# Ranks of equal keys counted at the end of diffusion step 1, and step 2 begun with its logits

## The chip, the core and the metric

The kernel runs on one core of one Trainium2 chip. The metric is the device time of one execution in microseconds (us); shown times are medians over several executions. The engines are named as in the profile: PE is TensorE's matmul, PEld its weight load, DVE is VectorE, ACT is ScalarE, POOL is GpSimd, SP is SyncE, which issues most of the DMAs. "PSUM" is the small memory into which PE writes and from which ACT and DVE read.

## What is computed

The input is `x` with 2708 rows of 512 values and an adjacency matrix of 2708 x 2708. A graph-attention layer comes first. The second layer, in which the change lies, normalises its input to `X` and then runs two diffusion steps:

```python
for s in range(STEPS):                       # STEPS = 2
    A = _adj_from_feats(Xa, W1, W2, W3)      # 2708 x 2708, from the rows of Xa
    Xf = Rf @ Xf                             # Rf, Rb: the adjacency S + I, scaled by rows or columns
    Xb = Rb @ Xb
    Xa = A @ Xa
    Z = Z + (Xf @ U1[s] + Xb @ U2[s] + Xa @ U3[s])
```

`_adj_from_feats` forms logits `Q @ W2 @ K.T`, sorts every row, keeps the largest entries whose softmax mass reaches 0.9, and takes a softmax over those kept. The sort is stable: of entries that are exactly equal, the one with the smaller column comes first. Columns with identical keys have identical logits in every row, so in step 2 the kernel forms for each column its **rank among equal keys**: how many columns before it hold the same key.

## The kernel before

Rows are cut into 22 tiles of 128 (the last has 20 rows). Two tiles form a pair (11 pairs), four a quad (6 quads, the last of two tiles). The loop over `s` at L946 runs step 1 (`s` = 0) and step 2 (`s` = 1, `last`). Inside a step all instructions of PE, ACT, DVE and SP run in the order in which the program writes them (`tc.manual_schedule`, L1230); POOL's order is left to a scheduler. The work of a step:

- **Keys.** L959 to L962 load the 2708 keys into `keys` (one buffer for both steps) in two slices, tiles 0 to 19 and the rest. `Logits.queries` (L516) loads a pair's queries on SP; `Logits.products` (L528) multiplies them with the keys on PE and copies six pieces of 452 columns per tile from PSUM into the tile's logits `p` on ACT. There are four buffers `p`, so two pairs.
- **Softmax of a pair.** `Logits.exp` (L541): on DVE the maxima `nmx` (L564), on ACT two exponentials a tile (L571, L578), on POOL the trial thresholds (`points`, L581 to L591), and then, if asked for, twelve "looks" on ACT that measure the mass at three thresholds, and `masses` on POOL (L594 to L596). For the first pair DVE measures these masses itself (L714 to L716).
- **Search.** `search` (L704) finds each row's threshold: four rounds of a point and a measure over both tiles (L650), then `finish` (L836), which writes the kept entries into `keep`. All of it is DVE work. Its last part is a branch for rare rows (L928 to L935). Its arguments `early` and `late` are pieces of other work that are written between the rounds and ahead of `finish`. The second round begins with the next-but-one pair's maximum.
- **A @ Xa.** `attended` (L1078): PE transposes `keep` in groups of four tiles (L1089), ACT copies them (`at`, L1093), PE multiplies them with the values `va` (L1111), six groups for each of a pair's two tiles.
- **Xf, Xb.** `part` (L975): a list of small work steps, two parts for each quad. In step 2 a part is 22 products of a block of S (`s_r`) with rows of `fhl_d` or `bhl_d` (`hl`), four multiplications with U (L1023), and four `summed` (L1037), which read PSUM on ACT and add on POOL (L1048). Each product loads 256 KB and 512 KB on SP. Such lists are run in bites by `paced` (L1073) as `others`; small ACT work of the next pair runs likewise as `fills`.

At the end of step 1 the last pair's `attended` runs, then `mixed` (L1134), which projects the new rows into step 2's keys and queries (`kq_d`), multiplies by U3 and stores `xa_d` and `y_d`.

Step 2 then begins with `ranks` (L1180). PE weighs all keys with a ramp into one number a column (L1194, six pieces, copied by ACT into `same`), transposes that row for the tiles' own numbers (L1199, `own`), and DVE compares: for tile `t` one instruction over `t` times 128 columns and its own counts the equal ones before each column (`counted`, L1210, into `rk`). After the ranks come the first pair's logits, its maxima and exponentials, all of part 0, and the loads of `va` on SP (L969). In the loop over `g` at L1250, `g` = -1 is the search of the first pair, with the second pair's `products`, `spread` (L1214: the ranks go through PE, ACT and two DMAs into every partition as `rank`), 11 of the 19 steps of the second pair's `exp`, and part 1. `g` = 0 begins with the third pair's `products`, whose buffers `p` are those of the first pair; the second pair's other looks follow between groups of the first pair's `attended`, ahead of the second pair's search.

Of the kernel before, what the change touches and what calls it, by code (L numbers as in the profile page):

```python
# [24 lines left out]
P = 128  # L25
# [28 lines left out]
def kernel(  # L54
# [36 lines left out]
    G = 2  # L91
# [37 lines left out]
    def row_bcast(ap, n):  # L129
        return bass.AP(tensor=ap.tensor, offset=ap.offset, ap=[[0, P], [1, n]])  # L130
# [812 lines left out]
    va = big.tile([P, NT, D], F32, name="va")  # L943

    keys = big.tile([P, N], F32R, name="keys")
    for s in range(STEPS):  # L946
        last = s == STEPS - 1
        with ExitStack() as st:
# [7 lines left out]
            ps_a = st.enter_context(tc.tile_pool(name=f"s{s}psa", bufs=2, space=PSUM, reuse_waits="tile"))  # L956
            ps_s = st.enter_context(tc.tile_pool(name=f"s{s}pss", bufs=1, space=PSUM, reuse_waits="tile"))

            h = (NT - NT % G - G) * P  # L959
            for c in (slice(0, h), slice(h, N)):  # L960
                for i in range(2):
                    nc.sync.dma_start(out=keys[i * DA:(i + 1) * DA, c].bitcast(F32), in_=kq_d[s][:DA, i, c])  # L962
            if last:
                also = st.enter_context(tc.tile_pool(name="s1also", bufs=1))
            rank = also.tile([P, N], BF16, name="rank") if last else None

            def values():
                for t in range(NT):
                    nc.sync.dma_start(out=va[:rows[t], t, :], in_=(xa_d if last else va_d)[cols[t], :])  # L969

            if last:
                g_b = also.tile([P, D], F32, name="g_b")
# [204 lines left out]

                return rest

            def ranks(junk):  # L1180

                same = wide.tile([P, N], F32, name="keep")
                mask = wide.tile([P, N], F32, name="keep").bitcast(BF16)[:, :(NT + 1) * P]
                own = small.tile([P, NT], F32, name="own", bufs=1)
                rk = small.tile([P, NT], F32, name="rk", bufs=1)
                ramp = sp.tile([P, 2 * G * P], F32R, name="s_r")[:, :P]
                nc.vector.tensor_copy(ramp, down.to_broadcast([P, P]))
                nc.vector.memset(mask[:, :NT * P], 1.0)  # L1190
                nc.vector.tensor_copy(mask[:, NT * P:], below_d)
                for c0, c1 in chunks:
# [3 lines left out]
                for cs in tgroups:  # L1196
# [3 lines left out]
                    full = [c for c in cs if rows[c] == P]  # L1200
                    for r, c0, c1 in ((P, cs[0], cs[0] + len(full)), (rows[cs[-1]], cs[0] + len(full), cs[-1] + 1)):
                        if c0 < c1:
                            nc.scalar.copy(own[:r, c0:c1], pt[:r, c0 - cs[0]:c1 - cs[0], 0])

                def counted(ts):
                    for t in ts:
                        pr = rows[t]
                        w = t * P + pr
                        o = (NT - t) * P
                        nc.vector.scalar_tensor_tensor(junk[:pr, :w], same[:pr, :w], own[:pr, t:t + 1],  # L1210
                                                       mask[:pr, o:o + w], op0=OP.is_equal, op1=OP.mult,
                                                       accum_out=rk[:pr, t:t + 1])

                def spread():  # L1214
                    pt = ps_t.tile([P, TG, P], F32, name="t")
                    nc.tensor.transpose(pt[:NT, 0], rk, ident)
                    rk_t = sp.tile([P, 2 * G * P], F32R, name="s_r").bitcast(BF16)[:NT, :P]
                    nc.scalar.copy(rk_t, pt[:NT, 0])
                    nc.sync.dma_start(out=rank_d.rearrange("(t p) -> t p", p=P), in_=rk_t)
                    nc.sync.dma_start(out=rank, in_=row_bcast(rank_d, N))  # L1220

                nc.vector.memset(rk, 0.0)
                counted(range(NT // 2))
                return lambda: counted(range(NT // 2, NT)), spread

            pools = (wide, small, ps_t)
            NP = len(pairs)
            with tc.manual_schedule(engines={PE, ACT, DVE, SP}):  # L1230
                junk = wide.tile([P, -(-N // 4) * 2], F32, name="junk", bufs=1)
                counted, spread = ranks(junk.bitcast(BF16)[:, :N]) if last else (None, None)
# [3 lines left out]
                steps = lg[0].exp(looks=False)  # L1236
                if last:
# [12 lines left out]
                for g in range(-1, NP):  # L1250

                    fills = []

                    others = part(half, g + 2)
                    if g + 2 < NP:
                        lg[g + 2].products()
                    if g < 0:
                        paced(left, len(left))
                    if g + 3 < NP:
                        lg.append(Logits(pools, s, pairs[g + 3], keys, rank))  # L1260
                        lg[g + 3].queries()
# [12 lines left out]
                    def early(g=g):  # L1274
                        if g + 2 < NP:
                            fills.extend(lg[g + 2].exp())
                        first, *more = lg[g + 2].maxima if g + 2 < NP else [lambda: None]

                        def begin():
                            paced(pending, len(pending))  # L1280
                            first()

                        return begin, lambda: [x() for x in more], lambda: [rest() for rest in norms]

                    def late(g=g):
                        if g >= 0:
                            out_ = rest_of(att)
                            if last:
                                done.extend(zip(pairs[g], out_))
                            else:  # L1290
                                mixed(pairs[g], out_, others, fills, final)
                            keeps = min(len(others), len(quads[g // 2 + 1])) if last and others else 0
                            while len(others) > keeps or fills:
                                paced(others, min(2, len(others) - keeps))
                                paced(fills, 1)
                            left.extend(others)
                            others.clear()
                            return


                        if last:
                            spread()
                        if last:
                            paced(fills, 5 + G * NA)
                            paced(others, len(others))
                        else:
                            paced(others, 1)
                            paced(fills, 2 * G + 1)
                            while others:
                                paced(others, KD + 1)  # L1310
                                paced(fills, G)
                        looks.extend(fills)

                    if g + 1 < NP:
                        opened = None
                        if g >= 0:
                            opened = Opened(lg[g + 1], True, junk)
                            opened.bracket()
                        ready = search(lg[g + 1], opened, junk, early, late)
                    else:  # L1320
                        for rest in norms:
                            rest()
                        paced(pending, len(pending))
                        late()
# [35 lines left out]
```

## Time and profile before

| what | us or count |
|---|---|
| time, median of 3 runs (3669.59 to 3671.01) | 3670.35 |
| the profiled execution: time / its span | 3677.04 / 3675.3 |
| PE busy in the span | 3333.6 (91%) |
| DVE busy | 2653.8 (72%) |
| ACT busy / POOL busy | 1500.3 (41%) / 841.9 (23%) |
| first matmul of step 2 starts at | 2320.77 |
| `L1210`, the 22 counts of ranks, first to last start | 2325.0 to 2361.7 |
| `va<-xa_d` issued on SP, 22 loads of 256 KB | 2390.5 to 2405.0 |

The table's times within the execution are counted from the start of the span. An engine's share is a mean over stages: at the end of step 1 PE is full and DVE has little to do, at the start of step 2 it is the other way round. A line of the timeline gives the start, the duration, the engine, the line of the kernel, what is written and read, and in brackets the idle time of that engine just before it and what ended it.

### The profile page before, as it was taken

The page shows a single profiled execution, that of the slowest core. Times are in us where ns is not written, and L with a number is a line of the kernel's source. Part 1 is how long each engine was busy: PE and PEld are TensorE (multiplying, and loading weights), DVE is VectorE, ACT ScalarE, POOL GpSimd, SP SyncE. Part 2 cuts the span into 40 slices and gives each one's busy share as a digit, 9 for nine tenths or more (in the row PEclk, how much of TensorE's full clock was granted, in tenths as well). Part 3 has the DMA queues.
Part 4 walks back from the last instruction along what each step waited for, and adds up shares of the span by engine and source line. Part 5 has one row for each costly group of instructions (what it writes and reads, how often), then busy time and mean ns, then how long its engine had stood idle before and what let it go on. Part 6 is the DMA issues. An engine that isn't in the chain of part 4 may idle for free. (4 is left out here: it accounts for less than half of the span.)

```text
span 3675.3 us, 33992 instructions
## 1 busy us (share of the span) xinstructions
PE 3333.6 (91%) x10791; PEld 1728.0 (47%) x10791; DVE 2653.8 (72%) x4829; ACT 1500.3 (41%) x2248; POOL 841.9 (23%) x1028
## 2 busy tenths in 40 slices
PE   8998999998967789999999999877989999999977
PEld 4433333333444454645555454553555555565533
DVE  4587888989965465546463653595989988889984
ACT  2343212011113466566565651234545644455600
POOL 4114240514321012112221221111122222122211
PEclk9999999999979889999999999988999999999989
DMA  3477424233227343625444352782465445565433
GB/s 117 150 253 246 139 79 154 76 105 100 84 80 269 131 162 110 217 71 193 147 148 170 133 174 89 237 292 73 160 215 199 161 171 201 179 233 186 160 118 130
DMA packets 249298, 579.99 MB, mean 158 GB/s; under 512 B 33293, under 2 KB 67037, under 8 KB 244833
## 3 DMA queue, kind: packets, MB, share of 16 engines
q1 hardware_dynamic: 229749, 509.14, 41.7%
q0 software_dynamic: 19328, 68.33, 4.8%
q8 instruction: 86, 1.41, 0.2%
q14 instruction: 135, 1.11, 0.1%
HBM read 471.68 MB, written 105.68 MB: 157 GB/s over the span
## 5 line engine op out<-in xcount | busy, mean ns | idle before, releaser
L1111 PE MATMUL a<-va,at 128*128 128x512 f32 (+2 forms) x1936 | 895.1, 602 | 16.0 <-ACT at L1093 15.8
L442 PE MATMUL po<-e,fw 128*65 128x512 f32 (+4 forms) x2112 | 835.8, 551 | 36.3 <-DVE e L440 21.5
L440 DVE SCALAR_TENSOR_TENSOR e<-r_b,kk,a_c 128x512 f32<-128x512 f32 (+4 forms) x1056 | 749.7, 739 | 73.4 <-PE po L442 23.7
L571 ACT ACTIVATE junk_a<-p,nth 128x2708 uint8<-128x2708 f32 (+1 forms) x240 | 612.7, 2553 | 55.5 <-POOL nth L586 51.2
L1002 PE MATMUL q<-hl,s_r 128*128 128x512 f32 x1936 | 529.2, 423 | 72.5 <-DMA s_r<-s_d 72.4
L442 PEld LDWEIGHTS po<-e,fw 128*65 128x65 f32 (+1 forms) x2112 | 285.7, 139 | 546.2 <-issue 269.4
L1111 PEld LDWEIGHTS a<-va,at 128*128 128x128 f32 (+2 forms) x1936 | 340.9, 188 | 390.5 <-issue 337.0
L1002 PEld LDWEIGHTS q<-hl,s_r 128*128 128x128 f32 x1936 | 367.0, 193 | 223.9 <-issue 57.6
L650 DVE SCALAR_TENSOR_TENSOR junk<-p,th 128x2708 bf16<-128x2708 f32 (+1 forms) x132 | 423.1, 3205 | 3.3
L1093 ACT COPY at<-t 128x512 f32<-128x512 f32 (+3 forms) x308 | 140.1, 476 | 491.9 <-PE t L1089 490.7
L1023 PE MATMUL q<-u_k,tt 128*128 128x512 f32 x704 | 321.3, 599 | 10.7 <-DMA u_k<-in_L_gnn_U_dram 10.7
L538 ACT COPY p<-t 128x452 f32<-128x452 f32 (+2 forms) x264 | 130.9, 537 | 406.6 <-PE t L536 352.4
L1005 PE MATMUL q<-s_r,hl 128*128 128x512 f32 (+1 forms) x1056 | 280.8, 410 | 12.2 <-DMA s_r<-s_d 12.2
L536 PE MATMUL t<-keys,q_t 128*128 128x452 f32 x528 | 159.4, 431 | 87.2 <-ACT p L538 73.2
L1005 PEld LDWEIGHTS q<-s_r,hl 128*128 128x128 f32 x1056 | 186.7, 188 | 99.9 <-issue 53.0
L1023 PEld LDWEIGHTS q<-u_k,tt 128*128 128x128 f32 x704 | 135.3, 192 | 162.6 <-issue 147.6
L846 DVE MAX8 vn<-keep 128x8 f32<-128x2708 f32 (+1 forms) x66 | 196.8, 2981 | 2.3
L564 DVE TENSOR_REDUCE nmx<-p 128x1 f32<-128x2708 f32 (+1 forms) x44 | 130.5, 2967 | 69.6 <-ACT p L538 69.6
L424 ACT ACTIVATE s_c<-a_c 128x512 fp32r<-128x512 f32 (+3 forms) x132 | 76.2, 577 | 250.1 <-DMA a_c<-in_adj_t_dram 124.0
L1089 PE MATMUL t<-ident,keep 128*128 128x128 f32 (+1 forms) x968 | 148.6, 276 | 31.7 <-DVEq L933 15.8
L1089 PEld LDWEIGHTS t<-ident,keep 128*128 128x128 f32 (+1 forms) x968 | 115.4, 141 | 123.5 <-issue 89.7
L1151 PE MATMUL a<-u_k,v_t 128*128 128x512 f32 (+1 forms) x352 | 169.8, 619 | 3.3 <-DMA u_k<-in_L_gnn_U_dram 3.3
(304 smaller groups left out, 3289.1 us busy)
## 6 DMA issues: line engine op xcount, KB each, us to landing
s_r<-s_d SPq DMA_DIRECT2D x330, 256.0 KB
hl<-vhl_d SPq DMA_DIRECT2D x132, 512.0 KB
hl<-fhl_d SPq DMA_DIRECT2D x132, 512.0 KB
hl<-bhl_d SPq DMA_DIRECT2D x132, 512.0 KB
u_k<-in_L_gnn_U_dram SPq DMA_DIRECT2D x184, 256.0 KB
arow<-in_adj_dram SPq DMA_DIRECT2D x21, 1354.0 KB
s_d<-s_c SPq DMA_DIRECT2D x88, 256.0 KB
a_c<-in_adj_t_dram SPq DMA_DIRECT2D x84, 256.0 KB
```

What stands on the lines that cost most here:

```text
L440: nc.vector.scalar_tensor_tensor(e[:pr, :cw], r_b[:pr, i, :cw], kk[:pr, t, hd:hd + 1], a_c[t][:pr, :cw], op0=OP.max, op1=OP.mult)
L442: nc.tensor.matmul(po[i][:, :cw], lhsT=fw[:pr, t, hd, :], rhs=e[:pr, :cw], start=(t == 0), stop=(t == NT - 1))
L536: nc.tensor.matmul(pl[:, :c1 - c0], lhsT=q[:, i], rhs=self.keys[:, c0:c1], start=(i == 0), stop=(i == 1))
L571: nc.scalar.activation(junk[:pr], self.p[i][:pr], func, **kw)
L650: nc.vector.scalar_tensor_tensor(self.junk_b[:pr], p, th, p, op0=OP.is_ge, op1=OP.mult, accum_out=dst)
L846: v.max(vs, keep[0][:pr])
L1002: nc.tensor.matmul(half[j], lhsT=s_r[:, j * P:(j + 1) * P], rhs=hl[:, h], start=(c == 0 and h == 0), stop=(c == NT - 1 and h == 1))
L1005: nc.tensor.matmul(half[j][:, :w], lhsT=hl[:, h, j * P:(j + 1) * P], rhs=s_r[:, :w], start=(c == 0 and h == 0), stop=(c == NT - 1 and h == 1))
L1023: nc.tensor.matmul(half[j], lhsT=across_t[-1][:, k, j * P:(j + 1) * P], rhs=u_k, start=(start and k == 0), stop=(start and k == KD - 1))
L1089: nc.tensor.transpose(pt[:rows[c], j, :pr], keep[i][:pr, cols[c]], ident[:pr, :pr])
L1111: nc.tensor.matmul(pa[:pr], lhsT=at[:rows[c], j, :pr], rhs=va[:rows[c], c, :], start=(c == 0), stop=(c == NT - 1))
L1151: nc.tensor.matmul(pz[i][:rows[t]], lhsT=v_t[i][:, k, :rows[t]], rhs=u_k, start=(k == 0), stop=(k == KD - 1))
```

## The change

At the end of step 1, in its last `attended`, the ranks of tiles 0 to 17 are formed (`early_tiles` is 18): their keys are loaded in the loop's last round, and a new function `ranked` gives the ramp, the key pieces and the transposes as a list of steps, which run as `fills` from the second group on, and the counts, which follow as one. In step 2 `ranked` runs for tiles 18 to 21 alone, after the first pair's logits; its counts come after that pair's maxima. `own` and `rk` now outlive a step. The mask is set by GpSimd. The loads of `va` in step 2 are issued by GpSimd, ahead of the ranks. After half of part 0's steps (11 of its list) come `spread` and the second pair's `products`, then the rest of part 0. All of the second pair's exponentials and looks are written into `g` = -1.

```diff
-            h = (NT - NT % G - G) * P
-            for c in (slice(0, h), slice(h, N)):
+            def asked(s, c):
                 for i in range(2):
                     nc.sync.dma_start(out=keys[i * DA:(i + 1) * DA, c].bitcast(F32), in_=kq_d[s][:DA, i, c])
+
+            if not last:
+                asked(s, slice(0, early_tiles * P))
+            asked(s, slice(early_tiles * P, N))
...
-            def values():
+            def values(queue):
                 for t in range(NT):
-                    nc.sync.dma_start(out=va[:rows[t], t, :], in_=(xa_d if last else va_d)[cols[t], :])
+                    queue.dma_start(out=va[:rows[t], t, :], in_=(xa_d if last else va_d)[cols[t], :])
...
+            def ranked(junk, ts, name, bufs):
+                end = ts[-1] * P + rows[ts[-1]]
+                same = wide.tile([P, N], F32, name=name, bufs=bufs)
+                mask = wide.tile([P, N], F32, name=name, bufs=bufs).bitcast(BF16)[:, :(NT + 1) * P]
                 ramp = sp.tile([P, 2 * G * P], F32R, name="s_r")[:, :P]
+                def begin():
+                    nc.vector.tensor_copy(ramp, down.to_broadcast([P, P]))
+                    nc.gpsimd.memset(mask[:, :NT * P], 1.0)
+                    nc.gpsimd.tensor_copy(mask[:, NT * P:], below_d)
+                def piece(c0, c1):
                     pl = ps_t.tile([P, 512], F32, name="t")
                     nc.tensor.matmul(pl[:, :c1 - c0], lhsT=ramp, rhs=keys[:, c0:c1], start=True, stop=True)
                     nc.scalar.copy(same[:, c0:c1], pl[:, :c1 - c0])
+                def owned(cs):
                     pt = ps_t.tile([P, TG, P], F32, name="t")
                     for j, c in enumerate(cs):
                         nc.tensor.transpose(pt[:rows[c], j], same[:, cols[c]], ident)
+                        nc.scalar.copy(own[:rows[c], c:c + 1], pt[:rows[c], j, :1])
+                def counted(t):
+                    pr = rows[t]
...
+                steps = [begin]
+                steps += [lambda a=(c0, min(c1, end)): piece(*a) for c0, c1 in chunks if c0 < end]
+                steps += [lambda cs=ts[n:n + TG]: owned(cs) for n in range(0, len(ts), TG)]
+                return steps, [lambda t=t: counted(t) for t in ts]
...
                 if last:
-                    counted()
-                for step in lg[0].maxima + steps:
+                    values(nc.gpsimd)
+                    heads, counts = ranked(junk.bitcast(BF16)[:, :N], list(range(early_tiles, NT)), "keep", 2)
+                    paced(heads, len(heads))
+                for step in lg[0].maxima + steps + counts:
                     step()
...
-                for step in part(half, 0):
-                    step()
-                values()
+                others = part(half, 0)
+                if last:
+                    paced(others, NT // 2)
+                    spread()
+                    lg[1].products()
+                paced(others, len(others))
+                if not last:
+                    values(nc.sync)
...
-                    if g + 2 < NP:
+                    if g + 2 < NP and not (last and g < 0):
                         lg[g + 2].products()
...
+                    if g == NP - 1 and not last:
+                        asked(s + 1, slice(0, early_tiles * P))
+                        heads, counts = ranked(junk.bitcast(BF16)[:, :N], list(range(early_tiles)), "p", 4)
+                        fills += heads + [lambda: paced(counts, len(counts))]
...
-                        att = attended(pairs[g], *ready, fills, others, 3 if g else len(tgroups) + 1)
+                        att = attended(pairs[g], *ready, fills, others, 1 if final else 3 if g else len(tgroups) + 1)
...
                         if last:
-                            spread()
-                        if last:
-                            paced(fills, 5 + G * NA)
+                            paced(fills, len(fills))
                             paced(others, len(others))
```

More of the change, by code (lines that the diff above doesn't have):

```diff
@@ L945 @@
     keys = big.tile([P, N], F32R, name="keys")
+    early_tiles = pairs[-2][0]
+    own = big.tile([P, NT], F32, name="own")
+    rk = big.tile([P, NT], F32, name="rk")
+    nc.vector.memset(rk, 0.0)
     for s in range(STEPS):
@@ L1178, in normed @@
                 return rest
[L1180 to L1187, printed above, removed]
-                ramp = sp.tile([P, 2 * G * P], F32R, name="s_r")[:, :P]
[L1189 to L1192, printed above, removed]
+            def ranked(junk, ts, name, bufs):
+                end = ts[-1] * P + rows[ts[-1]]
+                same = wide.tile([P, N], F32, name=name, bufs=bufs)
+                mask = wide.tile([P, N], F32, name=name, bufs=bufs).bitcast(BF16)[:, :(NT + 1) * P]
+                ramp = sp.tile([P, 2 * G * P], F32R, name="s_r")[:, :P]
+                def begin():
[3 more added lines that the diff above has]
+                def piece(c0, c1):
                     pl = ps_t.tile([P, 512], F32, name="t")
@@ L1195, in ranks @@
                     nc.scalar.copy(same[:, c0:c1], pl[:, :c1 - c0])
-                for cs in tgroups:
+                def owned(cs):
                     pt = ps_t.tile([P, TG, P], F32, name="t")
@@ L1199, in ranks @@
                         nc.tensor.transpose(pt[:rows[c], j], same[:, cols[c]], ident)
[L1200 to L1222, printed above, removed]
@@ L1223, in ranks @@
-                counted(range(NT // 2))
-                return lambda: counted(range(NT // 2, NT)), spread
+                        nc.scalar.copy(own[:rows[c], c:c + 1], pt[:rows[c], j, :1])
+                def counted(t):
+                    pr = rows[t]
+                    w = t * P + pr
+                    o = (NT - t) * P
+                    nc.vector.scalar_tensor_tensor(junk[:pr, :w], same[:pr, :w], own[:pr, t:t + 1],
+                                                   mask[:pr, o:o + w], op0=OP.is_equal, op1=OP.mult,
+                                                   accum_out=rk[:pr, t:t + 1])
@@ new lines, in ranked, with spread @@
+                steps = [begin]
+                steps += [lambda a=(c0, min(c1, end)): piece(*a) for c0, c1 in chunks if c0 < end]
+                steps += [lambda cs=ts[n:n + TG]: owned(cs) for n in range(0, len(ts), TG)]
+                return steps, [lambda t=t: counted(t) for t in ts]
+            def spread():
+                pt = ps_t.tile([P, TG, P], F32, name="t")
+                nc.tensor.transpose(pt[:NT, 0], rk, ident)
+                rk_t = sp.tile([P, 2 * G * P], F32R, name="s_r").bitcast(BF16)[:NT, :P]
+                nc.scalar.copy(rk_t, pt[:NT, 0])
+                nc.sync.dma_start(out=rank_d.rearrange("(t p) -> t p", p=P), in_=rk_t)
+                nc.sync.dma_start(out=rank, in_=row_bcast(rank_d, N))
@@ L1231 @@
                 junk = wide.tile([P, -(-N // 4) * 2], F32, name="junk", bufs=1)
-                counted, spread = ranks(junk.bitcast(BF16)[:, :N]) if last else (None, None)
                 lg = [Logits(pools, s, grp, keys, rank) for grp in pairs[:1]]
@@ L1236 @@
                 steps = lg[0].exp(looks=False)
+                counts = []
                 if last:
-                    counted()
-                for step in lg[0].maxima + steps:
+                    values(nc.gpsimd)
+                    heads, counts = ranked(junk.bitcast(BF16)[:, :N], list(range(early_tiles, NT)), "keep", 2)
+                    paced(heads, len(heads))
+                for step in lg[0].maxima + steps + counts:
                     step()
```

## The prediction, made before the result

> **What bounds the kernel now.** The page's busy shares (PE 91%, DVE 72%) are means over stages, so I read the stage that the change touches: first the busy time by windows of 20 us across the seam of the two steps, then the timeline there with the idle time in brackets, then the waits of PE, then the start of every round of the loop over g in step 2.
>
> ```profile
> 2250.00:2270.00 20.00, 19.67 (x60) 9.49 (x60) 0.08 (x1) 3.91 (x7) 5.37 (x8) 1.00 0.59 168
> 2270.00:2290.00 20.00, 20.00 (x66) 6.72 (x65) 0.00 (x0) 2.61 (x9) 0.00 (x0) 1.00 0.00 0
> 2290.00:2310.00 20.00, 19.23 (x59) 5.74 (x57) 0.00 (x0) 3.01 (x10) 3.85 (x9) 1.00 0.16 45
> ...
> 2330.00:2350.00 20.00, 16.79 (x68) 11.82 (x68) 19.43 (x21) 3.92 (x8) 0.00 (x0) 1.00 0.56 194
> ```
>
> The columns are PE, PEld, DVE, ACT, POOL, clock, DMA share, GB/s. At the end of step 1 PE is full, DVE has nothing to do and the DMAs rest; at the start of step 2 DVE is full and PE has gaps.
>
> ```profile
> 2325.02 0.35 DVE L1210 SCALAR_TENSOR_TENSOR junk<-keep,own 128x128 bf16<-128x128 f32 x1 [74.90 <-ACT own L1203]
> ...
> 2361.73 3.03 DVE L1210 SCALAR_TENSOR_TENSOR junk<-keep,own 20x2708 bf16<-20x2708 f32 x1
> ...
> 2364.70 5.84 DVE L564 TENSOR_REDUCE nmx<-p 128x1 f32<-128x2708 f32 x2
> ...
> 2381.89 3.04 DVE L650 SCALAR_TENSOR_TENSOR junk<-p,th_a 128x2708 bf16<-128x2708 f32 x1 [11.35 <-POOL th_a L587]
> ...
> 2403.60 2.87 PE L536 MATMUL t<-keys,q_t 128*128 128x452 f32 x6 [6.70 <-ACT p L538]
> ...
> 2419.70 8.09 PE L1002 MATMUL q<-hl,s_r 128*128 128x512 f32 x24 [8.15 <-DMA s_r<-s_d]
> ...
> 2503.96 6.72 PE L536 MATMUL t<-keys,q_t 128*128 128x452 f32 x16 [17.85 <-ACT p L538]
> ...
> 2534.48 0.17 DVE L658 TENSOR_TENSOR pts<-top,pts 128x6 f32<-128x6 f32 x1 [30.94 <-POOL pts L596]
> ```
>
> DVE spends 39.7 us on counts (2325.0 to 2364.7), then 5.8 on maxima, then waits 11.4 for exponentials. Its search ends at 2503.4, and only then PE gets the third pair's buffers: a wait of 17.85 us. Then DVE itself waits 30.9 us for the looks.
>
> ```profile
> 2503.37 0.97 ACT L538 COPY p<-t 128x452 f32<-128x452 f32 x2 [14.49 <-DVEq L928]
> ...
> 2630.86 0.97 ACT L538 COPY p<-t 128x452 f32<-128x452 f32 x2 [24.97 <-DVEq L928]
> ...
> 2750.54 0.97 ACT L538 COPY p<-t 128x452 f32<-128x452 f32 x2 [36.40 <-PE t L536]
> ...
> 2859.43 0.97 ACT L538 COPY p<-t 128x452 f32<-128x452 f32 x2 [33.95 <-PE t L536]
> ...
> 2972.88 0.97 ACT L538 COPY p<-t 128x452 f32<-128x452 f32 x2 [36.11 <-PE t L536]
> ...
> 3411.76 0.97 ACT L538 COPY p<-t 128x452 f32<-128x452 f32 x2 [33.90 <-PE t L536]
> ```
>
> These are the first copies of rounds g = 0, 1, 2, 3, 4 and 8. The first two were released by DVE's branch, all later ones by PE. The six rounds from 2750.54 to 3411.76 take 110.2 us each, the first two 127.5 and 119.7. So PE sets the pace from g = 2 on, and what is won is what PE wins by then; DVE's further lead is lost in waits.
>
> **What the Trainium skill says.** "TensorE: Matmul & The Clock Gate", Part 1: after an idle window of about 3.4 us the clock is halved until the array has again been busy that long. The trace agrees: after the gap of 8.15 us 24 matmuls take 8.09 us, elsewhere 6.02. A long gap costs some 2 us more than itself. "GPSIMD Engine Reference", section 1: GpSimd shares its SBUF access with VectorE instructions that have two SBUF inputs. The trace agrees: beside the adds of L1048 (9.32 us for four, else 1.27 each) an L650 takes 3.91 instead of 3.04. "SBUF — State Buffer", "SBUF: two separate sides", warns that some VectorE operations keep GpSimd from writing the descriptors of its DMAs. This trace shows no such delay: GpSimd's stores of `xa_d` and `y_d` take 0.52 to 0.67 us to issue in a step in which DVE is mostly busy. "DMA: Bandwidth & Descriptors", "SWDGE vs HWDGE vs iDMA": both kinds of queue feed the same 16 engines in turn, so `va` on GpSimd takes bandwidth from SP's loads if they coincide.
>
> **The change, part by part.** I call T the end of step 1 on PE (2320.8 before).
>
> *End of step 1, PE.* Added are 6 key matmuls (L1194, 0.47 each) and 18 transposes (22 took 2.69 us with their waits). They share two PSUM buffers with the transposes of `attended`, so a second step in a group waits for a copy of 0.59: 6 x 0.45 + 18 x 0.12 + 5 x 0.45 = 7.1. ACT (3.9 of 20 us busy) and DVE have room. The 18 counts are 39.7 less the last four (2361.73 + 3.03 - 2352.81 and a read: 12.0), 27.7 us within 66 idle ones. The keys of tiles 0 to 17 no longer wait for tile 19's store (4.9 us of waits at L962), and SP has issued `mixed`'s loads by about 2251, so they should land by 2259, just when PE asks. I take 8 in all. Ends: 4 if the steps hide in wait times, 13 if `va` disturbs the `u_k` loads, on which PE already waits 3.3 us there.
>
> *Start of step 2, DVE.* The first pair's products take 7.5 us (2326.86 to 2334.4), then six key pieces 3.4 and four transposes 0.7. Maxima end at T+10.8. ACT finishes products, pieces and `own` at T+12.3, its four exponentials take 11.0 (2367.7 to 2378.7), POOL's points 3.1: masses start at T+26.6, and the four counts (12.0) fit into DVE's wait. Before, it was T+61.1. From there to the end of the search took 121.5 us (2381.9 to 2503.4): DVE ends at T+148.1.
>
> *Start of step 2, PE.* Products and ranks 11.6. Part 0 took 61.6, of it 5.5 waits for loads. In the middle `spread` 0.6 and the second pair's products 7.5. SP's loads queue behind `spread`'s two DMAs, as before; but that wait (8.15, and 7.8 from the first DMA's issue at 2411.9 to the next matmul) now runs beside those products, so 1 remains, and 3 for lost prefetch. Then part 1 follows at once: two of its accumulators are freed only after POOL's adds, 7.3 us after part 0 ends, less 1.5 of work: 5.8. This is the same cause as the 6.70 above, so that gap only moves. Part 1 is 56.1 of matmuls plus 1.5. Sum: 11.6 + 61.6 + 8.1 + 4 + 5.8 + 57.6 = 148.7, and 3.6 for the copies of `summed` that ACT does ahead of the next logits (2485.3 to 2488.9): T+152.3. DVE's T+148.1 is earlier, so PE is late next. Before: 2503.4 - 2320.8 = 182.6. **Gain 30.3.** If DVE should be later than reckoned, each us beyond 4 counts in full.
>
> *Rounds 0 and 1.* All 12 looks (2.7 us each, 32.4) now run in g = -1: ACT is free from about T+93, exponentials and points to T+108, looks to T+141, before DVE asks at T+148. So DVE's 30.9 us wait goes, and with it PE's 5.35 at 2631 and the delay of SP's store at L1176, behind which PE waited 6.89 at 2672.9. Both rounds should come to the 110.2 of the others: 127.5 + 119.7 - 220.4 = 26.8. I take 24. Ends: 10 and 28.
>
> *Values.* 22 x 0.26 MB = 5.8 MB, at the 340 GB/s of full windows 17 us of all DMA engines. A tile of `va` is free once PE's last groups have read it (about 2285 to 2298), with idle DMAs; but POOL's order is the scheduler's, and if the loads go after its last adds (2324) they meet part 0's loads. GpSimd's issue, 22 x 0.55 = 12 us, is then done by T+17, before the points. Not visible in the trace; 0 to 8, and I take 4. SP loses 14.8 us of issues, which were not the last cause of a wait.
>
> Step 1's start: the keys' second slice and the queries still wait for layer 0's last tiles (PE waits 13.4 for `q_t` there): 0.
>
> **Sum:** 30.3 + 24 - 8 - 4 = 42.3. The execution took 3677.0, so 3634.7; it lies 6.7 above the median of 3670.35, so on that scale **3628**.
>
> **The rivals.**
> *DMA takes the wait's place.* From T to round 0 the parts' 34.6 MB, `va` 5.8 and about 6 of `tt`, `u_k`, `z` and ranks must come; at the windows' 294 to 339 GB/s that is 137 to 158 us against PE's 152. For it: DMA share 0.87 to 0.99 there already. Against: prefetch starts before T, and `va` may come early. At the slow end some 12 us more stalls: 3640.
> *PE gains only round 0.* The two early rounds stay long, because ACT's exponentials, which start only at the seventh group, hold up the copies for PE (4.21 at 2559), and step 1 pays 12: 30.3 + 8 - 12 - 4 = 22, so 3648. Against: the steady rounds have the same exponentials at 110.2.
> *Slower: GpSimd's queue.* If every load is held until a gap between DVE's instructions, 22 of them stand ahead of the mask and the points. At 4 us each (one 3 us operation and an issue) from T+4 the points end at T+95, DVE at T+216.6, 34 later than before; the looks' 24 come back, step 1's 8 are paid: 18 slower, 3688. It decides from 3.2 us a load. Against it: the issue times above.
>
> **How the numbers follow.** Forecast 0.58, DMA 0.14, less gain 0.14, GpSimd's queue 0.08; the remaining 0.06 is for something unseen, half of it slower and half no change. A measurement of this kernel tells 0.2% (7 us) from no change. So faster 0.86, same 0.03, slower 0.11. The forecast's own range, from its ends, is 3612 to 3642. The range of 3610 to 3652 takes in the two weaker gains.
>
> **What would show it.** DVE busy with L1210 between 2270 and 2315; some 8 us more until step 2's first logits; masses starting 27 us after them; no gap of 17.85 or 30.94; rounds 0 and 1 near 110, later rounds unchanged with more DVE waits at L564. It would be wrong if masses start later than T+35, if PE waits for `s_r` in part 0 by more than 15 us in all, or if the first two rounds stay above 118.

## The result, and the profile after

The changed kernel takes **3628.4 us** (median of 4 runs, 3623.33 to 3630.61) against 3669.97 for the kernel before (4 runs, 3668.27 to 3671.01). The ratio is **0.9885**, with a 95% interval of 0.9868 to 0.9902. The profiled execution took 3630.61 us with a span of 3628.7; the one before had 3677.04 and 3675.3.

The line numbers below are those of the changed kernel: the counts are now at L1216 (before L1210), the copies of the own keys at L1210 (before L1203), the products with S at L1009 (before L1002), the transposes of `attended` at L1096. "T" is again the first matmul of step 2; it starts at 2328.58 now and started at 2320.77 before.

First the busy times by windows of 20 us (columns as in the prediction: PE, PEld, DVE, ACT, POOL, clock, DMA share, GB/s).

```profile
2270.00:2290.00 20.00, 17.50 (x43) 6.09 (x43) 15.85 (x23) 3.30 (x18) 1.39 (x3) 0.74 0.05 14
2290.00:2310.00 20.00, 19.23 (x66) 5.83 (x66) 10.22 (x11) 2.30 (x8) 12.27 (x21) 1.00 0.79 250
...
2330.00:2350.00 20.00, 17.17 (x54) 10.26 (x54) 14.66 (x9) 15.54 (x28) 3.35 (x5) 0.83 0.54 197
```

DVE, idle here before, is busy for 15.9 and 10.2 us with counts. But PE falls from 20.0 to 17.5 us in the first window and its granted clock from 1.00 to 0.74: step 1's end pays for the counts. In the second window the DMAs work where they rested, and POOL is busy for 12.3 us: the loads of the values.

Then the timeline of the changed kernel at the places that were shown of before.

```profile
2268.74 0.35 DVE L1216 SCALAR_TENSOR_TENSOR junk<-p,own 128x128 bf16<-128x128 f32 x1 [30.27 <-ACT own L1210]
...
2287.48 0.55 POOL L976 DMA_DIRECT2D va<-xa_d  x1 [35.03 <-PE a L1118]
...
2306.55 0.54 POOL L976 DMA_DIRECT2D va<-xa_d  x1 [0.32 <-PE a L1118]
...
2332.91 2.97 DVE L564 TENSOR_REDUCE nmx<-p 128x1 f32<-128x2708 f32 x1 [32.27 <-ACT p L538]
...
2349.97 3.03 DVE L1216 SCALAR_TENSOR_TENSOR junk<-keep,own 20x2708 bf16<-20x2708 f32 x1
...
2357.34 3.04 DVE L650 SCALAR_TENSOR_TENSOR junk<-p,th_a 128x2708 bf16<-128x2708 f32 x1 [4.34 <-POOL th_a L587]
...
2475.18 0.17 DVE L939 RECIPROCAL rden<-den 128x2 f32<-128x2 f32 x1 [3.45 <-DVEq L928]
...
2484.31 0.96 ACT L538 COPY p<-t 128x452 f32<-128x452 f32 x2
...
2484.89 1.12 PE L536 MATMUL t<-keys,q_t 128*128 128x452 f32 x4 [2.32 <-ACT p L538]
...
2582.76 0.17 DVE L658 TENSOR_TENSOR pts<-top,pts 128x6 f32<-128x6 f32 x1 [1.92 <-POOL pts L596]
...
2595.43 0.97 ACT L538 COPY p<-t 128x452 f32<-128x452 f32 x2 [24.13 <-PE t L536]
...
2705.22 0.97 ACT L538 COPY p<-t 128x452 f32<-128x452 f32 x2 [34.69 <-DVE fr L690]
...
2814.77 0.97 ACT L538 COPY p<-t 128x452 f32<-128x452 f32 x2 [34.58 <-PE t L536]
...
3367.67 0.97 ACT L538 COPY p<-t 128x452 f32<-128x452 f32 x2 [34.15 <-PE t L536]
```

The masses start at T+28.8 (before T+61.1). The first search ends at 2475.18, T+146.6. PE begins its third pair only after that, at 2481.58, and the pair's first copy, with which round 0 begins, comes at T+155.7: the wait of 17.85 us for the search is gone (2.32 remain, for ACT), and PE is the late one. The wait of 30.94 us for the looks is gone too; one round later 1.92 remain. Rounds 0 and 1 take 111.1 and 109.8 us (127.5 and 119.7 before). 20 of the 22 loads of the values are issued before T, 0.54 us each.

The spans set against each other, with the prediction's terms:

| stretch | predicted | measured (before, after) |
|---|---|---|
| start to step 1's last `attended` | 0 | -5.8 (2253.95, 2248.11) |
| end of step 1 on PE | +8 | +13.65 (66.82, 80.47) |
| T to the first copy of round 0 | -30.3 | -26.9 (182.60, 155.73) |
| rounds 0 and 1 | -24 | -26.3 (247.17, 220.91) |
| values on GpSimd | +4 | no stretch of its own; no stall found |
| rounds 2 to 7 (first copy of round 2 to that of round 8) | 0 | +1.2 (661.22, 662.45) |
| from round 8's first copy to the end | 0 | -2.5 (263.54, 261.03) |
| sum | -42.3 | -46.6 |

Each span is that of one profiled execution, and spans scatter. In three executions of the experiments whose program is the changed kernel's up to round 0 (after_products_twice, after_measure_twice and measure_twice_stores_later), T to the first copy of round 0 took 149.8, 150.8 and 157.0 us. The end of step 1 took 78.5 to 84.0 us in the seven executions that have the changed kernel's copies there. A few us in one such span are not a finding.

### The profile page after: what moved, and what is told of

It reads as the page before. It is cut to its first block, busy times and chain, and to the rows that moved or that the text cites. A ratio compares the mean times of both kernels' runs of the same rounds, so it can differ in the third digit from the quotient of the medians.

```text
span 3628.7 us, 34073 instructions
## 1 busy us (share of the span) xinstructions
PE 3334.1 (92%) x10797; PEld 1718.8 (47%) x10797; DVE 2652.9 (73%) x4828; ACT 1505.5 (41%) x2269; POOL 854.2 (24%) x1054
## 5 line engine op out<-in xcount | busy, mean ns | idle before, releaser
L440 DVE SCALAR_TENSOR_TENSOR e<-r_b,kk,a_c 128x512 f32<-128x512 f32 (+4 forms) x1056 | 750.8, 739 | 71.6 <-PE po L442 21.6
L1009 PE MATMUL q<-hl,s_r 128*128 128x512 f32 x1936 | 525.9, 420 | 66.9 <-DMA s_r<-s_d 65.1
L1009 PEld LDWEIGHTS q<-hl,s_r 128*128 128x128 f32 x1936 | 363.1, 191 | 219.7 <-issue 59.7
L1012 PE MATMUL q<-s_r,hl 128*128 128x512 f32 (+1 forms) x1056 | 280.6, 410 | 11.6 <-DMA s_r<-s_d 11.3
L564 DVE TENSOR_REDUCE nmx<-p 128x1 f32<-128x2708 f32 (+1 forms) x44 | 130.6, 2968 | 104.4 <-ACT p L538 104.4
L1096 PE MATMUL t<-ident,keep 128*128 128x128 f32 (+1 forms) x968 | 147.8, 275 | 29.4 <-DVEq L933 13.9
L1096 PEld LDWEIGHTS t<-ident,keep 128*128 128x128 f32 (+1 forms) x968 | 115.0, 140 | 121.8 <-issue 86.6
```

The costliest lines, as they stand in the source:

```text
L440: nc.vector.scalar_tensor_tensor(e[:pr, :cw], r_b[:pr, i, :cw], kk[:pr, t, hd:hd + 1], a_c[t][:pr, :cw], op0=OP.max, op1=OP.mult)
L1009: nc.tensor.matmul(half[j], lhsT=s_r[:, j * P:(j + 1) * P], rhs=hl[:, h], start=(c == 0 and h == 0), stop=(c == NT - 1 and h == 1))
L1012: nc.tensor.matmul(half[j][:, :w], lhsT=hl[:, h, j * P:(j + 1) * P], rhs=s_r[:, :w], start=(c == 0 and h == 0), stop=(c == NT - 1 and h == 1))
L1096: nc.tensor.transpose(pt[:rows[c], j, :pr], keep[i][:pr, cols[c]], ident[:pr, :pr])
```

## The experiments

All times are medians; the ratio is to the kernel before, run on the same chip, whose median was 3670.6 to 3672.8 us there; differences in us between runs are less exact by some 3. The changed kernel itself has 0.9885 [0.9868, 0.9902].

| run | us | ratio and 95% interval |
|---|---|---|
| own_in_groups | 3614.63 | 0.9843 [0.9829, 0.9857] |
| ranks_in_step2 | 3635.90 | 0.9905 [0.989, 0.992] |
| looks_left | 3655.02 | 0.9953 [0.9936, 0.9969] |
| second_pair_late | 3642.64 | 0.9925 [0.9905, 0.9945] |
| values_by_sync | 3638.36 | 0.9901 [0.9885, 0.9917] |
| before_all_looks | 3642.13 | 0.9917 [0.9905, 0.993] |
| groups_ranks_in_step2 | 3635.33 | 0.9894 [0.9877, 0.9912] |
| after_measure_twice | 3669.04 | 0.9992 [0.9982, 1.0001] |
| before_measure_twice | 3717.44 | 1.0119 [1.0102, 1.0135] |
| after_products_twice | 3643.01 | 0.9932 [0.9909, 0.9956] |
| measure_twice_stores_later | 3671.15 | 1.0000 [0.9991, 1.0008] |
| groups_stores_later | 3607.60 | 0.9831 [0.9817, 0.9844] |

**Why step 1's end costs 13.65 us.**

```diff
 def owned(cs):
     for j, c in enumerate(cs):
         nc.tensor.transpose(pt[:rows[c], j], same[:, cols[c]], ident)
-        nc.scalar.copy(own[:rows[c], c:c + 1], pt[:rows[c], j, :1])
+    full = [c for c in cs if rows[c] == P]
+    for r, c0, c1 in ((P, cs[0], cs[0] + len(full)), (rows[cs[-1]], cs[0] + len(full), cs[-1] + 1)):
+        if c0 < c1:
+            nc.scalar.copy(own[:r, c0:c1], pt[:r, c0 - cs[0]:c1 - cs[0], 0])
```

> The changed kernel with the own keys of a group of four tiles copied by ACT once per group, as before the change, and not tile by tile. Theory (step 1's end costs 13.65 instead of 8 because each of its transposes waits for the ACT copy of the one before): the three L1209 stretches shrink from 9.1 us to about 3, step 1's end on PE from 80.5 to 72 to 75 us, total 5 to 9 us less than the changed kernel (about 3621). Rival (the key pieces, the shared PSUM buffers and the slow clock there are the cost): the end of step 1 stays at 79 to 81 us, total within 2 us of 3628.

The timeline of PE there, first of the changed kernel, then of own_in_groups:

```profile
2268.18 0.33 PE L1209 MATMUL t<-ident,p 128*128 128x128 f32 x1 [0.54 <-ACT at L1100]
2268.76 0.33 PE L1209 MATMUL t<-ident,p 128*128 128x128 f32 x1 [0.25 <-ACT own L1210]
2269.34 0.33 PE L1209 MATMUL t<-ident,p 128*128 128x128 f32 x1 [0.25 <-ACT own L1210]
...
2277.70 3.78 PE L1118 MATMUL a<-va,at 128*128 128x512 f32 x4
...
2342.50 7.38 PE L1009 MATMUL q<-hl,s_r 128*128 128x512 f32 x24
```

```profile
2271.80 0.66 PE L1209 MATMUL t<-ident,p 128*128 128x128 f32 x4 [0.53 <-ACT at L1100]
...
2277.11 2.08 PE L1118 MATMUL a<-va,at 128*128 128x512 f32 x4
...
2336.16 5.72 PE L1009 MATMUL q<-hl,s_r 128*128 128x512 f32 x24
```

In the changed kernel every transpose waits for ACT to copy one column of the transpose before it: 0.58 us from one to the next. Copied once per group, four take 0.66 us together. And the four matmuls after the stretch take 2.08 us instead of 3.78. The windows of own_in_groups show the clock:

```profile
2270.00:2290.00 20.00, 19.36 (x75) 7.99 (x74) 14.75 (x25) 3.27 (x14) 4.32 (x8) 1.00 0.31 93
2290.00:2310.00 20.00, 19.23 (x57) 6.76 (x55) 13.17 (x13) 2.07 (x9) 12.75 (x23) 0.83 0.56 177
```

The granted clock is 1.00 where it was 0.74. It fell to half beside these transposes in all seven profiled executions with early counts and copies per tile, for some 3 to 14 us, and did not in the two with early counts and copies per group, nor at this place in the five without early counts. (The dip in the second window is another one: some 20 us before T the clock fell in eight of the fourteen profiled executions, before_measure_twice among them.) The Trainium skill, "TensorE: Matmul & The Clock Gate", "A second HAM failure mode: psum-queue depth-cycling", describes such a loss: frequent short idle times of PE between groups make PE's clock gate swing. The trace agrees in kind: no gap here exceeds 0.6 us. The grouped copies take away the gaps and shorten the stretch of transposes together, so the runs do not show which of the two brings the clock down.

Step 1's end falls from 80.5 to 72.5 us, as the theory had it. Step 2's first stretch, which the theory left out, is shorter too: from T to round 0 it is 147.6 us instead of 155.7. The copies account for some 3.5 of these 8.1 us: 2 us fewer in the one group of transposes there, and the 24 matmuls that follow it in 5.72 instead of 7.38. The rest is not shown to be theirs: with the copies per tile the stretch also took 149.8 us, and groups_stores_later, with the copies per group, took 150.1. The total is 13.8 us lower, with intervals that do not overlap.

**What the early counts are worth.** ranks_in_step2 moves all counts to step 2; groups_ranks_in_step2 does so with the grouped copies.

```diff
-heads, counts = ranked(junk.bitcast(BF16)[:, :N], list(range(early_tiles, NT)), "keep", 2)
+heads, counts = ranked(junk.bitcast(BF16)[:, :N], list(range(NT)), "keep", 2)
...
-heads, counts = ranked(junk.bitcast(BF16)[:, :N], list(range(early_tiles)), "p", 4)
-fills += heads + [lambda: paced(counts, len(counts))]
```

> The changed kernel with all 22 counts in step 2 after the first pair's maxima, none at the end of step 1; the early load of the keys, the loads by GpSimd, the place of the second pair and the looks stay. Theory (the early counts buy 28 us of VectorE but PE then waits for its own work, and step 1's end pays 13.65): step 1's end is back at 66 to 68 us, masses start 55 to 60 us after step 2's first matmul, the search ends some 175 us after it and PE's third pair waits for it 15 to 20 us; total only 5 to 14 us above the changed kernel (3633 to 3642). Rival (the early counts are the main gain of the change): 25 to 35 us above it (3653 to 3663).

> Own keys copied once per group, and all 22 counts in step 2 after the first pair's maxima: the pair of this run with own_in_groups (3614.6, same copies, 18 counts at the end of step 1) gives the worth of the early counts without the cost of the tile-by-tile copies on either side. Theory (the early counts save some 27 us of VectorE at the start of step 2, of which PE's own work there and the 6 to 8 us that they cost at the end of step 1 take back most): step 1's end is 66 to 67 us against 72.5, PE's third pair waits for VectorE's search until 168 to 174 us after step 2's first matmul against 147.6; total 12 to 20 us above own_in_groups (3627 to 3635). Rival (nearly all of the early counts' gain is lost, as 3636 against 3628 suggested): 5 to 10 us above it (3620 to 3625).

Step 1's end is back at 66.9 and 65.1 us, the masses start at T+53.1 and T+52.0, and VectorE's search ends last, at T+175.2 and T+173.2. The first copy of round 0 in ranks_in_step2 shows it; it waits for the branch at the end of the search:

```profile
2487.44 0.97 ACT L538 COPY p<-t 128x452 f32<-128x452 f32 x2 [8.50 <-DVEq L928]
```

Grouping gains nothing there, since PE is not the late one (3635.9 and 3635.3). So in the change as it stands the early counts gained 7 us by the medians, as the theory had it, but with overlapping intervals; with grouped copies they gain 20.7 (3635.3 against 3614.6, intervals apart), a little more than the 12 to 20 expected. With grouped copies the early counts pay for themselves; the tile-by-tile copies take two thirds of that back, and what is left is not clear of the noise.

**The looks**, left partly to g = 0 in the changed kernel (looks_left), and all taken ahead in the kernel before as the only edit (before_all_looks):

```diff
-paced(fills, len(fills))
+paced(fills, 5 + G * NA)
```

```diff
-paced(fills, 5 + G * NA)
+paced(fills, len(fills))
```

> The changed kernel with only the first 11 steps of the second pair's exponentials and looks in g = -1, the other looks in g = 0 as before the change. Theory (rounds 0 and 1 were long because VectorE waited for the looks): VectorE waits some 20 us at L658 again, rounds 0 and 1 come to 240 to 245 us together instead of 221, total 12 to 22 us above the changed kernel (3640 to 3650). Rival (they were long because the first search ended late): rounds stay at 219 to 225, total within 4 us of 3628.

> The kernel before the change with one edit alone: all looks of the second pair in g = -1. Theory (the looks are a share of the gain that needs no other part): VectorE's wait of 30.9 us at L658 goes, rounds 0 and 1 fall from 247 to 225 to 232 us, total 15 to 22 us below the kernel before (3648 to 3655). Rival (without the earlier first search the looks only move the wait to PE or to ACT's copies): within 5 us of the kernel before.

In looks_left the old wait is back, and larger than expected: VectorE's search ends early, at T+146.4, and then it stands for the looks that are left for g = 0.

```profile
2509.63 0.17 DVE L658 TENSOR_TENSOR pts<-top,pts 128x6 f32<-128x6 f32 x1 [33.90 <-POOL pts L596]
```

Its rounds 0 and 1 take 127.4 and 120.1 us, and the total is 26.6 above the changed kernel. In before_all_looks the first copies of rounds 0, 1 and 2 are:

```profile
2500.70 0.97 ACT L538 COPY p<-t 128x452 f32<-128x452 f32 x2 [14.49 <-DVEq L928]
...
2611.30 0.97 ACT L538 COPY p<-t 128x452 f32<-128x452 f32 x2 [23.41 <-PE t L536]
...
2721.04 0.97 ACT L538 COPY p<-t 128x452 f32<-128x452 f32 x2 [33.58 <-PE t L536]
```

Round 0 still starts after VectorE's branch, yet VectorE no longer waits at L658, and the two rounds take 110.6 and 109.7 us. This one edit gains 0.83% of the changed kernel's 1.15%. Both expectations underrated it; the mechanism stands and its rival falls.

**The place of the second pair**, put back after part 0:

```diff
-    paced(others, NT // 2)
-    spread()
-    lg[1].products()
...
-if g + 2 < NP and not (last and g < 0):
+if g + 2 < NP:
...
+    spread()
     paced(fills, len(fills))
```

> The changed kernel with the ranks' transpose and load and the second pair's products where they were before the change: after the first block of S. Theory (with early masses VectorE is at the second pair's maxima 62 us after step 2's first matmul, but these products would end only some 85 us after it): VectorE waits 18 to 25 us at L564 in the first search, which then ends 165 to 171 us after the first matmul, PE's third pair waits for it again by 5 to 12 us, and SP's wait for the ranks comes back before part 1 (5 to 8 us); total 9 to 18 us above the changed kernel (3637 to 3646). Rival (the move only reorders PE's work, and VectorE's lead covers it): within 4 us of 3628.

```profile
2413.74 2.97 DVE L564 TENSOR_REDUCE nmx<-p 128x1 f32<-128x2708 f32 x1 [21.61 <-ACT p L538]
```

This is VectorE at the second pair's maxima. It waits 21.6 us for the logits, its search ends at T+168.9, and round 0 starts there. The total is 14.2 us above the changed kernel, inside what the theory gave, and the rival falls.

**The values**, issued by SP after part 0:

```diff
-values(nc.gpsimd)
...
-if not last:
-    values(nc.sync)
+values(nc.sync)
```

> The changed kernel with the 22 loads of the values issued by SP after the first block of S, as before the change. Theory (their 14.8 us of issue and 5.8 MB then stand ahead of the second block's loads): PE waits 5 to 15 us more for s_r or hl at the second block's start, total 5 to 15 us above the changed kernel (3633 to 3643). Rival (a transfer that is hidden either way): within 3 us of 3628.

PE's timeline at the start of part 1, in this run and then in the changed kernel:

```profile
2436.38 7.33 PE L1009 MATMUL q<-hl,s_r 128*128 128x512 f32 x24 [17.14 <-DMA s_r<-s_d]
```

```profile
2416.63 1.90 PE L1009 MATMUL q<-hl,s_r 128*128 128x512 f32 x6 [2.01 <-DMA s_r<-s_d]
```

In the changed kernel the largest wait for loads there is 2.01 us. From T to round 0 the run takes 166.9 us, 11.2 more than the changed kernel and 9.9 more than the longest execution with the changed kernel's program there. The total is 10 above by the medians and 6 by the ratios, with overlapping intervals, so it is the wait of 17.14 us rather than the total that speaks against the rival. The 22 loads in SP's queue do cost; on GpSimd no wait for them was found.

**Which engine sets the rounds.** The doubled measurement adds VectorE work to both kernels, the doubled products add PE work to the changed one:

```diff
 o.measure()
+if s and it == 0 and not begins:
+    o.measure()
```

```diff
-for i in range(2):
+for i in (0, 1, 0, 1) if self.s and t >= pairs[2][0] else (0, 1):
     nc.tensor.matmul(pl[:, :c1 - c0], lhsT=q[:, i], rhs=self.keys[:, c0:c1],
```

> The changed kernel, with the first measurement of every search of step 2 but the first made twice: 6.1 us more VectorE work in each of ten rounds, same values. Theory (from g = 0 on PE sets the pace and VectorE has some 10 us of lead in each round): VectorE's waits at L564 fall from 104 to about 45 us, total 0 to 8 us above the changed kernel. Rival (the search is the pace): 6 us for each round, 50 to 60 us above it (3678 to 3688).

> The kernel before the change with the same doubled measurement. Theory (VectorE's waits at L564 were only 14.4 us in all, so its lead is used up at once; PE was the pace by about 2 us a round): 30 to 55 us above the kernel before (3700 to 3725). Rival (PE was the pace with room to spare in the later rounds as in the changed kernel): 0 to 15 us above it.

> The changed kernel with the logits' matmuls of every pair of step 2 from the third on made twice over (the second result replaces the first, same values): some 5.5 to 6 us more PE work in each of nine rounds and about 3 for the last, single-tile halves. Theory (PE sets the pace; the 40 us that the doubled measurement cost were the rounds with VectorE's branch and the tail, where VectorE was already at its limit): every round from 0 on grows by 5 to 6 us, plain ones too, total 45 to 60 us above the changed kernel (3673 to 3688), while VectorE's waits at L564 rise. Rival (the two engines pass the work to and fro, so that either one's extra work counts by about two thirds): 3 to 4 us a round, 28 to 40 us above it (3656 to 3668).

The products first. One pair's stretch at PE, in the run and in the changed kernel:

```profile
3041.99 10.39 PE L536 MATMUL t<-keys,q_t 128*128 128x452 f32 x48
```

```profile
3038.57 0.99 PE L536 MATMUL t<-keys,q_t 128*128 128x452 f32 x4
3039.78 1.11 PE L536 MATMUL t<-keys,q_t 128*128 128x452 f32 x4 [0.21 <-ACT p L538]
...
3046.29 1.09 PE L1096 MATMUL t<-ident,keep 128*128 128x128 f32 x8 [0.20 <-ACT p L538]
```

The plain stretch lasts 7.7 us (3038.57 to 3046.29), because PE waits for ACT's copy after every fourth matmul; the doubled one lasts 10.2 (3041.99 to 3052.22) without those waits. So the run added 2.5 us a round to PE, not 5.5 to 6, and the eight rounds from 0 to 7 grew by 2.4 on average (883.4 to 902.5 us; 1.0 to 3.6 each). VectorE's waits at L564 from round 2 on rose from 15.6 to 28.2 us. What PE really loses comes through in full: PE sets the pace of these rounds. The total, 14.6 higher, met neither expectation, since both took twice the matmuls for twice the time.

The measurement adds 6.1 us of VectorE work a round. It costs 44.7 us in the kernel before, within the theory's 30 to 55, and 40.6 in the changed one (by the medians), where the theory had 0 to 8 and the rival 50 to 60: neither fits. Of the 35.2 us by which rounds 1 to 7 grow in the changed kernel, 23.6 arise in two rounds (109.8 to 122.7, and 115.4 to 126.1); the other five grow by 0.9 to 4.6. The last stretch adds 10.1; PE waits there for VectorE's branch, 13.9 us already in the changed kernel and 15.8 here. VectorE's waits at L564 from round 2 on fall from 15.6 us to nothing, and the page's total for the line from 104.4 to 90.2, not to 45: most of that total lies in other stages. So the lead of VectorE was far smaller than the theory took it to be, and about as small in the kernel before (14.4).

In the first long round the waits of the queues and PE's timeline show how it gets to PE; the columns of the first line are the total, the number of waits and the longest:

```profile
SPq L1185 <- DVE yo L1184: 42.5, 2, 41.5
```

```profile
2635.73 3.40 PE L1011 MATMUL q<-hl,s_r 128*128 128x512 f32 x8 [9.94 <-DMA s_r<-s_d]
```

SP holds a store of the output for 41.5 us until VectorE has normalised those rows, and behind the store stand the loads of S for which PE then waits 9.94 us. In the changed kernel this wait of SP is 23.8 us in that round and PE waits 1.4 at most; in the kernel before it was 43.2, and PE waited 6.89. To test this path, both stores were moved behind three more products' loads, with the doubled measurement and, as a version that might be faster, with the grouped copies:

```diff
-if n == 4:
+if n == 9:
     paced(stores, len(stores))
```

> The changed kernel with the doubled measurement, and with the two stores of the output issued by SP before the tenth group of A @ Xa instead of the fifth, so that three products' loads go ahead of them. Theory (VectorE's extra 6 us reach PE through SP: the store waits for VectorE's last operation on the output, 41.5 us in the round of 122.7 us, and the loads of S behind it come 9.9 us late): PE's waits of 8 to 10 us for s_r in the two long rounds fall to 1 to 4, these rounds to 113 to 118, total 12 to 25 us below the doubled measurement alone (3644 to 3657); what remains is VectorE's own limit in the last rounds. Rival (VectorE's lateness reaches PE through the logits' buffers and the search): total within 5 us of 3669.

> The changed kernel with grouped own copies, and with the same later place of the stores. Theory: only the round with VectorE's branch (some 115 us against 109 to 110) and the small waits for s_r gain, 3 to 8 us in all below own_in_groups (3607 to 3612). Rival (the store's wait is covered in all rounds but that one, and its 6 us come from the branch itself): within 2 us of 3614.6.

With the doubled measurement the 9.94 us go and that round falls from 122.7 to 112.6. Rounds 0 to 7 together are 8.9 us shorter in the profile and the last stretch 2.4 longer, but the total stays (3671.15), and 12 to 25 less were expected: the theory of one path falls. The next long round keeps 125.5 us, now by another queue. ACT's and PE's timeline of measure_twice_stores_later:

```profile
2856.15 0.20 ACT L574 ACTIVATE nmx<-nmx 128x1 f32<-128x1 f32 x1 [9.63 <-DVE nmx L564]
...
2858.94 0.40 ACT L1102 COPY at<-t 128x128 f32<-128x128 f32 x2
...
2859.24 3.22 PE L1120 MATMUL a<-va,at 128*128 128x512 f32 x3 [6.45 <-ACT at L1102]
```

ACT stands 9.63 us before an exponential whose maximum VectorE has not formed, and the copy that PE needs stands behind it. So VectorE's lateness reaches PE through at least two queues, SP's and ACT's. The stretch from T to round 0 was 6.2 us longer here than without the moved stores (157.0 against 150.8). No store has moved up to there, so this is the scatter between executions named above.

With the grouped copies and no doubling, groups_stores_later takes the one round that stays long in the changed kernel, the one after VectorE's branch for ties (115.4 us), to 108.6: PE's longest wait for `s_r` there, 4.18 us in the changed kernel and 3.26 in own_in_groups, is 0.96. Its median of 3607.60 is the lowest of all, 7.0 below own_in_groups; the intervals of the two overlap, so the moved stores' share is not settled by the times. Both are faster than the kernel before and the changed one.

## Why the prediction was right, point by point

**The total.** The forecast of 3628.0 stands beside 3628.4. Part of the agreement is luck: the profile shows -46.6 us for the predicted -42.3, while the profiled execution of before lay 6.7 above its median and that of after 2.2 above its own. And the terms missed by up to 5.8 us and cancel in part: the end of step 1 and the start of step 2 came out 9.1 us worse in that execution, while values, rounds 0 and 1, and the first and the last stretch of the table, which were to stay as they were, came out 14.6 better.

**End of step 1, +8, measured +13.65.** The step was mis-sized. The term "18 x 0.12" came from the transposes of before, whose ACT copies went once per group of four. The changed `owned` copies tile by tile, as the diff shows, so a transpose costs 0.58 to 0.73 us; and the slower clock after such a stretch was not in the sum. From the first transpose to the end of A @ Xa 15.6 us were added where the sum had 7.1, and 2.0 came back in the waits for `u_k`. The waits of the key pieces were as predicted in size, 0.53 us where a second step in a group waits, though it did so three times and not five. The upper end of 13 was given for another cause, loads of values that disturb `u_k`; those waits fell instead, from 3.3 to 1.3. With grouped copies 5.8 stand for the 15.6, so the 7.1 fit the copies for which they were reckoned, and the whole added time is 5.6 (66.8 to 72.5).

**Start of step 2, VectorE.** Masses at T+26.6 became T+28.8, the search's end at T+148.1 became T+146.6. The counts' place (2270 to 2315 forecast) was 2268.7 to 2300.5 for the 18 early ones.

**Start of step 2, PE.** T+152.3 became T+155.7. With 149.8 to 157.0 in the other executions of the same program the sum holds within their scatter. PE was late next, not VectorE, as reasoned: in all four of these executions the search ended at T+146.1 to T+147.0, ahead of round 0. Some terms missed. Products and ranks took 13.9 for 11.6, because of the tile-by-tile copies, and 24 matmuls after them ran at the slower clock. Part 1 with the gap ahead of it took 67.0 for 63.4: until its accumulators were free PE waited 3.6 us (2.0 of them for a load) and not 5.8, but then 5.0 for loads, where the sum had 1.5 (before it was 5.8), and 26 matmuls took 8.30 us at the slower clock. The feared loss behind `spread` and the products, 1 and 3 us, was 0.6.

**Rounds 0 and 1, 24, measured 26.3.** Right, and the cause with it: looks_left takes 26.6 us back. What the sum hid is that this part needs none of the others, since before_all_looks has it too. The parts do not add up: each of those that serve the start (early counts, second pair, values) costs 7 to 14 us by the medians when it alone is undone, because whichever of PE and VectorE is late decides.

**Values, 4, measured none.** Twenty of the 22 loads went out as `attended` released its tiles, 2287.5 to 2306.6, with idle DMAs, before T. This was the better of the two orders that the prediction left open.

**Later rounds unchanged.** Right (+1.2), and PE sets their pace. But the sign that was named, more waits of VectorE at L564 in those rounds, hardly appeared: from round 2 on they were 14.4 before and 15.6 after. The page's higher total for that line (104.4 against 69.6) is the wait before step 2's first maximum, 32.3 us, which stood at the first count before. That VectorE had a lead to lose in every round was the prediction's reading of those waits; the doubled measurement shows that the lead is a few us in most rounds and nothing in two.

**The rivals.** DMA: part 0 and part 1 together waited some 14 us for loads (6.8 and 7.0), but the third pair came at T+155.7, not 12 later. Only round 0 gained: no. GpSimd's queue: an issue took 0.54 us beside counts, far from the 3.2 that would have decided. The 5.8 us in the unchanged part of step 1 are not explained; its last `attended` began between 2243.1 and 2253.8 in the profiled executions of the other runs, so a difference of this size is within what executions show.

## What to carry to other kernels

A copy that is written per tile instead of per group is cheap on its own engine (0.16 us) and dear for the engine that waits on it, here 0.58 us a tile and a lower clock after it; look at the waits between two alternating engines before adding such a list to a full engine. When several edits relieve the same stage, undo them one at a time: the cheapest, a count of looks in one line, had most of the gain. An engine that is not the bound can still stop it through the in-order queue of a third one, here a store that SP holds with the next loads behind it.

## What the hardware showed that was not expected

- Doubling the logits' matmuls (24 more a pair) cost PE 2.5 us, since the hand-over between PE and ACT's copies set the pace of that stretch: PE waited some 0.2 us for a copy after every fourth matmul.
- Short transposes with gaps of 0.25 us were followed by matmuls at about half speed: in the changed kernel not after the first four of them, but after the next eight (3.78 us for four matmuls, else 2.08), with no gap above 0.6 us near them. In after_measure_twice the same four matmuls took 2.07 us, and the eight after six more transposes 5.12, else 3.61: where the clock falls differs between executions.
- GpSimd issued loads at 0.54 us each while VectorE counted (2287.5 to 2300.5).
- The stretch from T to round 0 took 149.8 to 157.0 us in four executions of one and the same program up to there.
